# Sides of the feed-forward norm made within self-attention, early squares added by VectorE, the next group's norm one chunk ahead

## The chip, the cores and the metric

The kernel runs on one NeuronCore of a Trainium2 chip. The metric is the device time of one execution in microseconds, from launch to end; a profile gives in addition the span from the first to the last instruction on the core. Five engines work side by side, each on its own instruction queue: TensorE (PE) does matmuls, VectorE (DVE) and ScalarE (ACT) work element by element, GpSimd (POOL) too, and SyncE (SP) starts transfers. They wait for one another by semaphores. Matmul results land in PSUM[...]; everything else lives in SBUF.

## The reference

One perceiver block on 32 sequences of 64 positions and width 512, with a context of 1601 positions for each sequence; all in fp32:

```python
x = x + xattn(layernorm(x), ctx_1024, mask, rms_scale, q_w, kv_w, out_w)   # 4 heads of 128, one key/value head
x = x + attn(layernorm(x), WQ, WK, WV, WO)                                 # 16 heads of 32, causal
x = x + ffn(layernorm(x), W_fc, ln_w, ln_b, W_proj)

def ffn(x, W_fc, ln_w, ln_b, W_proj):          # 512 -> 2048 -> 512
    h = x @ absmean(W_fc).T                    # absmean: weights to -1, 0, 1
    h = gelu(h)                                # the exact one
    h = layernorm(h) * ln_w + ln_b             # over the 2048 hidden values
    return h @ absmean(W_proj).T
```

The change concerns the third line and the seam between the second and the third.

## The kernel before

The 2048 rows of x (32 sequences of 64) are 16 tiles `xs[0..15]` of 128 rows by 512, and stay in SBUF throughout. Cross-attention comes first and is not touched. A branch on a value read at run time picks between two forms of it, each followed by `rest`, which holds self-attention and the feed-forward part.

**Self-attention** (`self_attention`) runs a loop over i, the 16 tiles. Two tiles form a group (GA = 2). In turn i it normalises the probabilities of tile i (`normalise`: L1051 to L1053), turns them with TensorE's transposes (`turn`: `aptp` L1063, copies `wo` L1068 shared by ScalarE and VectorE), multiplies by the values (`mix`: `po` L1076), makes the scores and the exponentials of tile i + 1 (`exponentials`: `sc` L1028, `s` L1033, `amx` L1042, GpSimd's subtraction L1043, ScalarE's exponential L1046) and puts out tile i (`self_out`: `aout` L1090, addition to x L1093). Between these steps a generator fills in matmuls: queries, keys and values of the next group, or, for the last group (turns 14 and 15), `first_hidden`, the first 12 chunks of the feed-forward part's hidden layer. In turns 5, 7, 9 and 11 `ffn_input` makes the normalised and turned input of the feed-forward part for tiles 0 to 3. The comparisons that turn the weights into -1, 0, 1 (`compare`) are also put into these turns. All of these matmuls rotate through three PSUM banks (`ps_m`, tag "mm", of the pool `as_m`); two SBUF buffers (`raw`, tag "raw") serve first the weight pieces and then the squares of `first_hidden`.

**The feed-forward part** works on groups of four tiles (GT = 4, so 512 rows), 16 chunks of 128 hidden values a group (FC = 16), 64 chunks in all. `hidden(n)` makes chunk n: 8 matmuls `fh` (L912, the input in two parts, `fxh` and `fxl`, a rounded one and its remainder), Gelu into `bank` (L920), the square `fsq` (L922), then two running sums for the inner norm: `sums[0]` of the values on GpSimd (L926), and `sums[1]` of the squares (L927) on the engine given as `adder`: `nc.gpsimd` for the 12 chunks of `first_hidden`, `nc.vector` for the rest. `split(n)` multiplies the chunk by `ln_w` and divides it into two parts `hTh` and `hTl` on VectorE (L1204, L1205), two chunks ahead; three buffers hold each part. Then 8 matmuls `y` (L1225) add the chunk to the four output tiles.

The norm over the 2048 hidden values is not applied to them. What it does is put in at the end: `y` is scaled by the reciprocal deviation, and two row vectors, the **sides**, are added: `ln_w` times `W_proj`, weighted by minus mean times reciprocal deviation, and `ln_b` times `W_proj`. They are made at the start of `feed_forward`: `ln_w` and `ln_b` are loaded, divided into two parts (`lnp`, L876 and L877), and 16 matmuls `sides` (L1151) give 4 rows, which VectorE copies to `side` (L1153). `spread` (L1159) makes 128 equal rows of each of the two with matmuls against a small constant `pick`, and ScalarE copies them to `Wwb` (L1160). `others` (L1193, L1194) adds them to x, GpSimd the second one, VectorE the first one. `measure` (`fst` L1170) makes mean and deviation from the sums at chunk 8 of each group.

`ffn_input(t)` for tiles 4 to 15 is called in the loop over n, at the chunks that `inputs_at` names. It calls `centred` (statistics L110, L112, L114, GpSimd's power L115, normalised `xn_f` L117; two buffers), four transposes (`ftp` L902) and the two parts (L876, L877).

The order on each engine's queue is the work of a planner in the kernel language: it takes the instructions in program order as their priority, and moves a ready one forward where it reckons that the engine would be idle and a buffer is free. So `lnw`, `lnb` load and many statistics run far ahead of their place in the text. Once the order is fixed, each queue is served in order, and an instruction that waits holds those behind it.

Of the kernel before, what the change touches and what calls it, by code (L numbers as in the profile page):

```python
# [18 lines left out]
F32 = mybir.dt.float32  # L19
I32 = mybir.dt.int32  # L20

F32R = mybir.dt.float32r
# [6 lines left out]
P = 128  # L29
B, T, D = 32, 64, 512  # L30
S = 1601
NT = B * T // P
# [7 lines left out]
GT = 4  # L40
# [40 lines left out]
def perceiver_kernel(ctx: ExitStack, tc: tile.TileContext, a: dict, out: bass.AP):  # L81
# [25 lines left out]
    def centred(src, gain, eps, name):  # L107

        stats = small.tile([P, 6], F32, tag="stats", name=f"stats_{name}")
        nc.vector.bn_stats(stats, src)  # L110
        mv = small.tile([P, 2], F32, tag="mv", name=f"mv_{name}")
        nc.vector.bn_aggr(mv, stats)  # L112
        rs = small.tile([P, 1], F32, tag="rs", name=f"rs_{name}")
        nc.vector.tensor_scalar(rs, mv[:, 1:2], gain, eps, ALU.mult, ALU.add)  # L114
        nc.gpsimd.tensor_tensor(rs, rs, neghalf[:, 0:1], ALU.pow)  # L115
        xn = norm.tile([P, D], F32, tag="xn", name=f"xn_{name}")
        nc.vector.tensor_scalar(xn, src, mv[:, 0:1], rs, ALU.subtract, ALU.mult)  # L117
        return xn
# [764 lines left out]
    def rest(store, measured):  # L883
        st = ExitStack()
        fw = st.enter_context(tc.tile_pool(name="fw", bufs=1))
        wf = fw.tile([P, DC, FF], F32R, name="wf")
        wp = fw.tile([P, FC, D], F32R, name="wp")
        lnw = fw.tile([P, FC], F32, name="lnw")
        lnb = fw.tile([P, FC], F32, name="lnb")
        sums = fw.tile([P, 2, D], F32, name="sums")  # L890
        first = [fw.tile([P, DC, GT * P], F32R, name=f"fx{k}_0") for k in ("h", "l")]

        so_far = [None, None]

        def slot(n):
            return bank[:, n % FC // 4, n % 4 * D : (n % 4 + 1) * D]

        def ffn_input(t, to, ps_t, t_tag):
            xn = centred(xs[t], 1.0, 1e-5, f"f{t}")
            tp = ps_t.tile([P, DC, P], F32, tag=t_tag, name=f"ftp_{t}")  # L900
            for c in range(DC):
                nc.tensor.transpose(tp[:, c, :], xn[:, c * P : (c + 1) * P], ident)  # L902
            at = slice(t % GT * P, (t % GT + 1) * P)
            halves(to[0][:, :, at], to[1][:, :, at], tp)

        def hidden(n, fx, ps_m, m_tag, squares, sq_tag, adder):

            cols = slice(n % FC * P, (n % FC + 1) * P)
            ps = ps_m.tile([P, GT * P], F32, tag=m_tag, name=f"fh_{n}")
            for i, part in enumerate(fx):  # L910
                for c in range(DC):
                    nc.tensor.matmul(  # L912
                        ps,
                        wf[:, c, cols],
                        part[:, c, :],
                        start=(i == 0 and c == 0),
                        stop=(i == 1 and c == DC - 1),
                    )
            g = slot(n)
            nc.scalar.activation(g, ps, AF.Gelu)  # L920
            sq = squares.tile([P, D], F32, tag=sq_tag, name=f"fsq_{n}")
            nc.scalar.activation(sq, g, AF.Square)  # L922
            if n % FC == 0:
                so_far[:] = g, sq
            else:
                nc.gpsimd.tensor_tensor(sums[:, 0], so_far[0], g, ALU.add)  # L926
                adder.tensor_tensor(sums[:, 1], so_far[1], sq, ALU.add)  # L927
                so_far[:] = sums[:, 0], sums[:, 1]

        with ExitStack() as sa:  # L930
            done = self_attention(sa, wf, wp, first, ffn_input, hidden, measured)
        feed_forward(st, wp, lnw, lnb, sums, first, slot, ffn_input, hidden, done, store)
        st.close()

    def self_attention(st, wf, wp, first, ffn_input, hidden, measured):

        raw = st.enter_context(tc.tile_pool(name="raw", bufs=2))
        p1 = st.enter_context(tc.tile_pool(name="a1", bufs=1))
# [71 lines left out]
        def first_hidden():  # L1010

            for n in range(12):
                hidden(n, first, ps_m, "mm", raw, "raw", nc.gpsimd)
                if n % 2:
                    yield

# [88 lines left out]
        for i in range(NT):  # L1105
            g, t = divmod(i, GA)
            if t == 0:
                steps = heads(g + 1, xT) if g + 1 < groups else first_hidden()
            next(steps)
            normalise(i, s)  # L1110
            next(steps)
            if t == 0 and g + 2 < groups:
                xns = centred_group(g + 2)
            turn(i, s)
            next(steps)
            oT = mix(i)
            if i + 1 < NT:
                s = exponentials(i + 1)
            self_out(i, oT)
            for j in chores.get(i, ()):  # L1120
                compare(raw, j, piece_of(j))
            if t == GA - 1 and g + 2 < groups:
                xT = turned_group(g + 2, xns)
            if i in (5, 7, 9, 11):
                ffn_input((i - 5) // 2, first, ps_m, "mm")
        return 12

    def feed_forward(st, wp, lnw, lnb, sums, first, slot, ffn_input, hidden, done, store):
        fx = st.enter_context(tc.tile_pool(name="fx", bufs=1))
        ft = st.enter_context(tc.tile_pool(name="ft", bufs=3))  # L1130
        fq = st.enter_context(tc.tile_pool(name="fq", bufs=2))
        f1 = st.enter_context(tc.tile_pool(name="f1", bufs=1))
        ps_m = st.enter_context(tc.tile_pool(name="fs_m", bufs=2, space=PSUM))
        ps_t = st.enter_context(tc.tile_pool(name="fs_t", bufs=2, space=PSUM))
        ps_y = st.enter_context(tc.tile_pool(name="fs_y", bufs=GT, space=PSUM))
        nc.scalar.dma_start(lnw, a["ln_w"])
        nc.scalar.dma_start(lnb, a["ln_b"])
        pick = f1.tile([4, 2, P], F32, name="pick")
        nc.scalar.dma_start(pick, a["pick"])
        second = [fx.tile([P, DC, GT * P], F32R, name=f"fx{k}_1") for k in ("h", "l")]  # L1140
        inputs = [first, second]
        G = NT // GT
        last = G * FC


        lnp = f1.tile([P, FC, 4], F32R, name="lnp")
        for k, src in enumerate((lnw, lnb)):
            halves(lnp[:, :, 2 * k], lnp[:, :, 2 * k + 1], src)
        sides = ps_t.tile([P, D], F32, tag="tp", name="sides")
        for c in range(FC):  # L1150
            nc.tensor.matmul(sides[:4], lnp[:, c, :], wp[:, c, :], start=(c == 0), stop=(c == FC - 1))  # L1151
        side = f1.tile([4, D], F32, name="side")
        nc.vector.tensor_copy(side, sides[:4])  # L1153
        Wwb = f1.tile([P, 2, D], F32, name="Wwb")

        def spread():
            for k in range(2):
                ps = ps_t.tile([P, D], F32, tag="tp", name=f"spread_{k}")
                nc.tensor.matmul(ps, pick[:, k, :], side, start=True, stop=True)  # L1159
                nc.scalar.copy(Wwb[:, k], ps)  # L1160

        stats = {}

# [42 lines left out]
            return hi, lo  # L1206


        inputs_at = {n: GT + k for k, n in enumerate((1, 3, 5, 7, 11, 14, 17, 20, 27, 30, 33, 36))}
        made, ys = done, None  # L1210
        ahead = [split(0), split(1)]
        spread()
        for n in range(last):
            g, c = divmod(n, FC)
            if c == 0:
                ys = [ps_y.tile([P, D], F32, tag="y", name=f"y_{g}_{t}") for t in range(GT)]
            if made < last and (n >= 8 or n % 2 == 0):
                hidden(made, inputs[made // FC % 2], ps_m, "mm", fq, "sq", nc.vector)
                made += 1
            if n + 2 < last:  # L1220
                ahead.append(split(n + 2))
            parts = ahead.pop(0)
            for t in range(GT):
                for i, part in enumerate(parts):
                    nc.tensor.matmul(  # L1225
                        ys[t],
                        part[:, t, :],
                        wp[:, c, :],
                        start=(c == 0 and i == 0),
                        stop=(c == FC - 1 and i == 1),  # L1230
                    )
            if c == 8:
                measure(g)
            if 10 <= c < 10 + GT:
                others(g, c - 10)
            if n in inputs_at:
                t = inputs_at[n]
                ffn_input(t, inputs[t // GT % 2], ps_t, "tp")
            if c == FC - 1:
                for t in range(GT):  # L1240
                    i = g * GT + t
                    nc.vector.scalar_tensor_tensor(
                        xs[i], ys[t], stats[g][0][:, t : t + 1], xs[i], ALU.mult, ALU.add
                    )
                    store(i)
# [108 lines left out]
```

## Time and profile before

| | us |
|---|---|
| time, median of 3 runs | 984.78 (983.76 to 987.26) |
| the profiled execution's own time | 985.89 |
| its span | 984.1 |
| PE busy | 906.7 (92%) |
| DVE busy | 651.9 (66%) |
| ACT busy | 306.8 (31%) |
| POOL busy | 293.1 (30%) |
| `hidden` chunk 0 starts (PE) | 685.1 |
| `sides` on PE, start and length | 730.5, 3.87 |
| first `fst` (chunk 8 of group 0) | 772.0 |
| mean granted clock of TensorE | 0.98 |

In the views that follow, L912 and the like are lines of the kernel; `y<-wp,hTh` means that `y` is written and `wp` and `hTh` are read; x16 is a count. PE and PEld are TensorE's matmuls and its weight loads, which overlap. A wait is read as "engine, what waits, line <- engine, what it waited for". Busy matmuls are partly overlapped, so their spacing (0.23 us for these of 512 columns) and not their length (0.39 us) is what a chunk of work costs.

### The profile page before, as it was taken

What the parts mean: (1) busy time and instruction counts of PE and PEld (TensorE: products, weight loads), DVE (VectorE), ACT (ScalarE), POOL (GpSimd) and SP (SyncE); (2) the same over time, 40 slices, a digit from 0 to 9 for tenths busy, and PEclk for the clock granted to TensorE, in tenths of its full rate; (3) what the DMA queues carried; (4) which work ended last, traced back from release to release, by engine and by line L of the source; (5) the groups of instructions that cost most, each with busy time, mean ns of one, the idle gap of its engine ahead of it and who ended that gap; (6) DMA issues with size and microseconds to landing.
All of it is one profiled execution on the core that took longest, in us unless ns stands there. A gap on an engine that the chain in (4) does not pass through costs nothing.

```text
span 984.1 us, 13369 instructions
## 1 busy us (share of the span) xinstructions
PE 906.7 (92%) x4694; PEld 672.1 (68%) x4694; DVE 651.9 (66%) x1209; ACT 306.8 (31%) x694; POOL 293.1 (30%) x264
## 2 busy tenths in 40 slices
PE   4997889999999999988989999999979899999995
PEld 2786667777677766755566766766647688888884
DVE  4994456656565443499976666666439798886864
ACT  1112345455454532122222222222622233333330
POOL 3554222323222221011011111111757454443330
PEclk9999899999999999999999999999999999999998
DMA  6266664876776550023310000000000010010101
GB/s 198 65 206 168 196 190 136 278 235 206 235 208 213 149 182 24 21 86 87 87 43 1 1 1 1 1 2 1 1 1 1 1 43 1 1 44 1 43 1 46
DMA packets 60964, 83.74 MB, mean 85 GB/s; under 512 B 11060, under 2 KB 34136, under 8 KB 60888
## 3 DMA queue, kind: packets, MB, share of 16 engines
q1 hardware_dynamic: 57568, 80.60, 27.3%
q10 hardware_dynamic: 3320, 2.20, 0.7%
q8 instruction: 39, 0.64, 0.3%
q14 instruction: 37, 0.30, 0.1%
HBM read 74.38 MB, written 4.19 MB: 80 GB/s over the span
## 4 chain that ended last, share of the span: by engine, by line
PE 62%; DVE 14%; POOL 4%; issue 3%; DMA 3%; ACT 3%; SPq 1%; POOLq 0%; DVEq 0%; ACTq 0%
PE y L1225 10%; PE fh L912 10%; PE kvp L382 9%; PE aV L1000 5%; PE xo L504 5%; PE aWQ L984 4%; PE aWK L984 4%; PE lgp L424 3%; PE enc L488 3%; DVE s L1033 3%; DMA nat<-in_ctx_dram 2%; PE aout L1090 2%; PE po L1076 1%; DVE amx L1042 1%; PE sc L1028 1%
## 5 line engine op out<-in xcount | busy, mean ns | idle before, releaser
L382 PE MATMUL kvp<-wkv,ct 128*128 128x256 f32 x576 | 140.8, 391 | 4.4 <-ACT kv L389 4.4
L382 PEld LDWEIGHTS kvp<-wkv,ct 128*128 128x128 f32 x576 | 111.5, 197 | 27.9 <-issue 7.3
L926 POOL TENSOR_TENSOR sums<-sums,bank 128x512 f32<-128x512 f32 x56 | 77.2, 1378 | 90.9 <-ACT bank L920 90.7
L1225 PE MATMUL y<-wp,hTh 128*128 128x512 f32 x256 | 102.7, 401 | 0.6 <-DVE hTh L1204 0.6
L1225 PE MATMUL y<-wp,hTl 128*128 128x512 f32 x256 | 100.7, 393 | 0.7 <-DVE hTl L1205 0.7
L1043 POOL TENSOR_TENSOR s<-s,amx 128x1024 f32<-128x1024 f32 x16 | 30.6, 1913 | 226.0 <-DVE amx L1042 226.0
L920 ACT ACTIVATE bank<-fh 128x512 f32<-128x512 f32 x64 | 38.1, 599 | 154.0 <-PE fh L912 154.0
L912 PE MATMUL fh<-fxh,wf 128*128 128x512 f32 x256 | 73.1, 407 | 6.3 <-issue 4.8
L912 PE MATMUL fh<-fxl,wf 128*128 128x512 f32 x256 | 71.4, 401 | 0.0
L1033 DVE SCALAR_TENSOR_TENSOR s<-sc,cmask 64x1024 f32<-64x1024 f32 x32 | 39.1, 1222 | 44.5 <-PE sc L1028 44.1
L927 DVE TENSOR_TENSOR sums<-sums,fsq 128x512 f32<-128x512 f32 x46 | 54.6, 1186 | 19.5 <-ACT fsq L922 19.4
L1000 PE MATMUL aV<-bank,axT 128*128 128x512 f32 x128 | 62.2, 631 | 4.4 <-DVE KT L991 4.4
L389 ACT ACTIVATE kv<-kvp,rstd 128x256 f32<-128x256 f32 x72 | 33.2, 469 | 92.8 <-PE kvp L382 54.6
L504 PE MATMUL xo<-wo,encT 128*128 128x512 f32 x128 | 59.7, 609 | 2.1 <-ACT encT L497 2.0
L1090 PE MATMUL aout<-bank,aoT 128*128 128x512 f32 x128 | 59.2, 605 | 0.7 <-ACT aoT L1084 0.7
L984 PE MATMUL aWQ<-axT,bank 128*128 128x256 f32 x256 | 58.3, 381 | 1.5 <-ACT axT L967 1.5
L912 PEld LDWEIGHTS fh<-fxh,wf 128*128 128x128 f32 x256 | 47.1, 190 | 18.3 <-issue 6.8
L1205 DVE SCALAR_TENSOR_TENSOR hTl<-bank,lnw,hTh 128x512 fp32r<-128x512 f32 x64 | 55.9, 874 | 5.3 <-PE y L1225 1.1
L191 PE MATMUL q<-xT,wq 128*128 128x256 f32 x256 | 58.2, 386 | 0.0
L984 PE MATMUL aWK<-axT,bank 128*128 128x256 f32 x256 | 57.9, 379 | 0.0
L1225 PEld LDWEIGHTS y<-wp,hTh 128*128 128x128 f32 x256 | 48.2, 188 | 13.8 <-DVE hTh L1204 1.4
L912 PEld LDWEIGHTS fh<-fxl,wf 128*128 128x128 f32 x256 | 48.9, 191 | 12.5 <-issue 0.8
(156 smaller groups left out, 1625.9 us busy)
## 6 DMA issues: line engine op xcount, KB each, us to landing
nat<-in_ctx_dram SPq DMA_DIRECT2D x64, 256.0 KB, 5.1
ct<-in_ctxT_dram SPq DMA_DIRECT2D x7, 768.0 KB, 4.8
xraw<-in_x_dram SPq DMA_DIRECT2D x16, 256.0 KB, 2.7
x<-in_x_dram SPq DMA_DIRECT2D x32, 128.0 KB, 4.9
qs<-bank SPq DMA_DIRECT2D x32, 128.0 KB, 3.1
raw_g<-in_W_fcT_dram SPq DMA_DIRECT2D x16, 256.0 KB, 3.7
raw_g<-in_W_projT_dram SPq DMA_DIRECT2D x16, 256.0 KB, 4.4
raw_q<-in_W_fcT_dram SPq DMA_DIRECT2D x16, 256.0 KB, 3.0
```

Source lines behind the costliest of these rows:

```text
L191: nc.tensor.matmul(ps.rearrange("p b t -> p (b t)"), wq[:, c, h, :], xT[:, c, :], start=(c == 0), stop=(c == DC - 1),)
L382: nc.tensor.matmul(ps.rearrange("p k h -> p (k h)"), cts[p][:, c, j * P : (j + 1) * P], wkv[:, c].rearrange("p k h -> p (k h)"), start=(c ...
L504: nc.tensor.matmul(o, encT[:, h].rearrange("p s t -> p (s t)"), wo[:, h, :], start=(h == 0), stop=(h == NH - 1),)
L912: nc.tensor.matmul(ps, wf[:, c, cols], part[:, c, :], start=(i == 0 and c == 0), stop=(i == 1 and c == DC - 1),)
L926: nc.gpsimd.tensor_tensor(sums[:, 0], so_far[0], g, ALU.add)
L927: adder.tensor_tensor(sums[:, 1], so_far[1], sq, ALU.add)
L984: nc.tensor.matmul(ps[:, m, :], ws[w][:, c, (m0 + m) * P : (m0 + m + 1) * P], xT[:, c, :], start=(c == 0), stop=(c == DC - 1),)
L1000: nc.tensor.matmul(ps, xT[:, c, i * P : (i + 1) * P], ws["WV"][:, c, :], start=(c == 0), stop=(c == DC - 1),)
L1033: nc.vector.scalar_tensor_tensor(s[half], sc[half, :, :, half].rearrange("p r m k -> p (r m) k"), DK**-0.5, cmask[half].unsqueeze(1).to_br ...
L1090: nc.tensor.matmul(ps, oT[:, c, :], ws["WO"][:, c, :], start=(c == 0), stop=(c == DC - 1))
L1205: nc.vector.scalar_tensor_tensor(lo, g, w, hi.bitcast(F32), ALU.mult, ALU.subtract)
L1225: nc.tensor.matmul(ys[t], part[:, t, :], wp[:, c, :], start=(c == 0 and i == 0), stop=(c == FC - 1 and i == 1),)
```

## The change

Four things, in one function after the other:

- The loads of `ln_w`, `ln_b` and `pick`, the division into `lnp`, the `sides` matmuls with their copy, and `spread` move from `feed_forward` to self-attention. The loads stand at the head of `rest`, `lnp` ahead of self-attention, `sides` at the end of turn 14 and `spread` at the end of turn 15. `sides` and `spread` use self-attention's "mm" banks; `side` takes one of the two "raw" buffers; `Wwb` no longer has SBUF of its own but lies in `wkv`, the key and value weights of cross-attention.
- The squares of the first 12 chunks are added by VectorE instead of GpSimd.
- `ffn_input` is cut in two: `ffn_input` is now the norm alone, `ffn_turned` the transposes and the two parts. In the loop over chunks the norm of a tile is called at one chunk and its turning at the next chunk.
- `inputs_at` names chunks 0, 2, 4, 6 in place of 1, 3, 5, 7 for the second group's tiles, so their turnings stay at chunks 1, 3, 5, 7. The others keep their chunk for the norm, and their turning goes one chunk later.

```diff
@@ rest
+        lnp = fw.tile([P, FC, 4], F32R, name="lnp")
+        pick = fw.tile([4, 2, P], F32, name="pick")
+        nc.scalar.dma_start(lnw, a["ln_w"])
+        nc.scalar.dma_start(lnb, a["ln_b"])
+        nc.scalar.dma_start(pick, a["pick"])
+
+        Wwb = wkv.rearrange("p c k h -> p (c k h)").rearrange("p (k d) -> p k d", k=2)
+
+        def sides(psum, tag, pool, s_tag):
+            ps = psum.tile([P, D], F32, tag=tag, name="sides")
+            for c in range(FC):
+                nc.tensor.matmul(
+                    ps[:4], lnp[:, c, :], wp[:, c, :], start=(c == 0), stop=(c == FC - 1)
+                )
+            side = pool.tile([P, D], F32, tag=s_tag, name="side")
+            nc.vector.tensor_copy(side[:4], ps[:4])
+
+            def spread():
+                for k in range(2):
+                    ps = psum.tile([P, D], F32, tag=tag, name=f"spread_{k}")
+                    nc.tensor.matmul(ps, pick[:, k, :], side[:4], start=True, stop=True)
+                    nc.scalar.copy(Wwb[:, k], ps)
+
+            return spread
...
-        def ffn_input(t, to, ps_t, t_tag):
-            xn = centred(xs[t], 1.0, 1e-5, f"f{t}")
+        def ffn_input(t):
+            return centred(xs[t], 1.0, 1e-5, f"f{t}")
+
+        def ffn_turned(t, xn, to, ps_t, t_tag):
             tp = ps_t.tile([P, DC, P], F32, tag=t_tag, name=f"ftp_{t}")
...
         with ExitStack() as sa:
+            for k, src in enumerate((lnw, lnb)):
+                halves(lnp[:, :, 2 * k], lnp[:, :, 2 * k + 1], src)
@@ self_attention
-                hidden(n, first, ps_m, "mm", raw, "raw", nc.gpsimd)
+                hidden(n, first, ps_m, "mm", raw, "raw", nc.vector)
...
             if i in (5, 7, 9, 11):
-                ffn_input((i - 5) // 2, first, ps_m, "mm")
+                k = (i - 5) // 2
+                ffn_turned(k, ffn_input(k), first, ps_m, "mm")
+            if i == NT - 2:
+                spread = sides(ps_m, "mm", raw, "raw")
+            if i == NT - 1:
+                spread()
@@ feed_forward
-        nc.scalar.dma_start(lnw, a["ln_w"])
-        nc.scalar.dma_start(lnb, a["ln_b"])
...
-        sides = ps_t.tile([P, D], F32, tag="tp", name="sides")
-        for c in range(FC):
-            nc.tensor.matmul(sides[:4], lnp[:, c, :], wp[:, c, :], start=(c == 0), stop=(c == FC - 1))
...
-        inputs_at = {n: GT + k for k, n in enumerate((1, 3, 5, 7, 11, 14, 17, 20, 27, 30, 33, 36))}
-        made, ys = done, None
+        inputs_at = {n: GT + k for k, n in enumerate((0, 2, 4, 6, 11, 14, 17, 20, 27, 30, 33, 36))}
+        made, ys, waiting = done, None, []
         ahead = [split(0), split(1)]
-        spread()
...
-            if n in inputs_at:
-                t = inputs_at[n]
-                ffn_input(t, inputs[t // GT % 2], ps_t, "tp")
+            for t, xn in waiting:
+                ffn_turned(t, xn, inputs[t // GT % 2], ps_t, "tp")
+            waiting = [(inputs_at[n], ffn_input(inputs_at[n]))] if n in inputs_at else []
```

More of the change, by code (lines that the diff above doesn't have):

```diff
@@ L930, in rest, with self_attention @@
         with ExitStack() as sa:
-            done = self_attention(sa, wf, wp, first, ffn_input, hidden, measured)
-        feed_forward(st, wp, lnw, lnb, sums, first, slot, ffn_input, hidden, done, store)
+            for k, src in enumerate((lnw, lnb)):
+                halves(lnp[:, :, 2 * k], lnp[:, :, 2 * k + 1], src)
+            done = self_attention(sa, wf, wp, first, ffn_input, ffn_turned, hidden, sides, measured)
+        feed_forward(st, wp, lnw, Wwb, sums, first, slot, ffn_input, ffn_turned, hidden, done, store)
         st.close()
-    def self_attention(st, wf, wp, first, ffn_input, hidden, measured):
+    def self_attention(st, wf, wp, first, ffn_input, ffn_turned, hidden, sides, measured):
         raw = st.enter_context(tc.tile_pool(name="raw", bufs=2))
@@ L1124, in self_attention, with feed_forward @@
             if i in (5, 7, 9, 11):
-                ffn_input((i - 5) // 2, first, ps_m, "mm")
+                k = (i - 5) // 2
[4 more added lines that the diff above has]
+                spread()
         return 12
-    def feed_forward(st, wp, lnw, lnb, sums, first, slot, ffn_input, hidden, done, store):
+    def feed_forward(st, wp, lnw, Wwb, sums, first, slot, ffn_input, ffn_turned, hidden, done, store):
         fx = st.enter_context(tc.tile_pool(name="fx", bufs=1))
@@ L1131, in feed_forward @@
         fq = st.enter_context(tc.tile_pool(name="fq", bufs=2))
-        f1 = st.enter_context(tc.tile_pool(name="f1", bufs=1))
         ps_m = st.enter_context(tc.tile_pool(name="fs_m", bufs=2, space=PSUM))
@@ L1135, in feed_forward @@
         ps_y = st.enter_context(tc.tile_pool(name="fs_y", bufs=GT, space=PSUM))
-        nc.scalar.dma_start(lnw, a["ln_w"])
-        nc.scalar.dma_start(lnb, a["ln_b"])
-        pick = f1.tile([4, 2, P], F32, name="pick")
-        nc.scalar.dma_start(pick, a["pick"])
         second = [fx.tile([P, DC, GT * P], F32R, name=f"fx{k}_1") for k in ("h", "l")]
@@ L1143, in feed_forward @@
         last = G * FC
-        lnp = f1.tile([P, FC, 4], F32R, name="lnp")
-        for k, src in enumerate((lnw, lnb)):
-            halves(lnp[:, :, 2 * k], lnp[:, :, 2 * k + 1], src)
-        sides = ps_t.tile([P, D], F32, tag="tp", name="sides")
-        for c in range(FC):
[L1151 to L1160, printed above, removed]
         stats = {}
```

## The prediction

> **What bounds the kernel now.** I read the busy time by stage first, then the chain that ended last in order of time, then the waits of the stage that looked worst, then the tiles concerned. The view by windows (window; busy time and count of PE, weight loads, DVE, ACT, POOL; granted clock; DMA share; GB/s):
>
> ```profile
> 684.00:703.00 19.00, 17.63 (x128) 12.68 (x127) 8.83 (x13) 12.06 (x20) 13.45 (x11) 1.00 0.00 1
> 703.00:722.00 19.00, 16.05 (x74) 11.29 (x76) 7.41 (x10) 9.59 (x17) 13.99 (x11) 0.95 0.00 1
> 722.00:738.00 16.00, 13.64 (x68) 6.57 (x59) 7.54 (x12) 2.69 (x5) 4.90 (x5) 0.95 0.00 0
> 738.00:772.00 34.00, 27.87 (x119) 21.42 (x118) 29.64 (x43) 4.99 (x9) 23.30 (x18) 0.95 0.00 1
> 772.00:834.00 62.00, 62.00 (x284) 50.43 (x283) 56.18 (x75) 20.08 (x33) 29.87 (x22) 1.00 0.08 17
> ```
>
> From 772 us on TensorE has no gap, and just before 684 us (attention of tiles 12 and 13) it has none either: 17.10 of 17.10 us busy in the window 651.4 to 668.5. Whatever moves the point at 772 us moves the end one for one; whatever the change does later than that is covered by a full TensorE. Between 684 and 772 us TensorE is idle or slow. The chain in order of time says on what (start, us, what):
>
> ```profile
> 713.95 1.25 POOL sums L927
> 715.28 1.27 POOL sums L927
> 716.58 0.63 ACT fsq L922
> ...
> 718.92 2.74 PE fh L912 x8
> 721.66 1.88 PE po L1076 x28
> ...
> 729.77 0.70 DVE x L1093
> 730.52 3.87 PE sides L1151 x16
> 734.39 0.93 PE fh L912 x4
> 735.32 1.91 PE spread L1159 x4
> 737.23 1.14 PE fh L912 x4
> ```
>
> GpSimd's additions of squares (L927) release ScalarE's squares, and only behind those come the copies that TensorE's `po` of the last tile needs. Then `sides` and `spread` lie open on the chain. The waits from 690 to 740 us (waiter, cause, total us, times, longest):
>
> ```profile
> ACT fsq L922 <- POOL sums L927: 5.0, 4, 1.9
> PE po L1076 <- ACT wo L1068: 2.8, 1, 2.8
> PE sides L1151 <- DVE x L1093: 1.7, 1, 1.7
> POOL x L1193 <- ACT Wwb L1160: 11.1, 1, 11.1
> ```
>
> The 738 to 772 window has another limit: DVE is busy 29.64 of 34 us. Its operations there are stretched while GpSimd works. The tiles (ns min/median/max, first and last start, forms), and the two lines of the timeline where it ends in an open stall of TensorE:
>
> ```profile
> L927 DVE TENSOR_TENSOR sums<-sums,fsq x46: 676/1287/1793, 741.2 to 955.8; 128x512 f32<-128x512 f32 x46
> L927 POOL TENSOR_TENSOR sums<-sums,fsq x10: 1263/1288/1447, 695.4 to 725.4; 128x512 f32<-128x512 f32 x10
> L1204 DVE TENSOR_SCALAR hTh<-bank,lnw x64: 470/475/1520, 724.2 to 968.2; 128x512 fp32r<-128x512 f32 x64
> ...
> 767.20 0.68 DVE L876 CAST fxh<-ftp 128x512 fp32r<-128x512 f32 x1
> 768.09 2.05 PE L912 MATMUL fh<-fxh,wf 128*128 128x512 f32 x4 [4.77 <-issue]
> ```
>
> **What the Trainium skill says.** "SBUF — State Buffer", section "Who interferes with whom": a DVE instruction in a two-port mode, or with two SBUF inputs beside a GpSimd instruction that reads SBUF, and GpSimd lock each other out for a whole instruction. The trace agrees: the same `hTh` takes 470 ns alone and up to 1520, the addition 676 and up to 1793. "GPSIMD Engine Reference", section 3.1: the addition is about twice as slow on GpSimd as on VectorE; here 1288 against 676 ns. "TensorE: Matmul & The Clock Gate", Part 1: an idle window of about 3.4 us halves the clock; the granted clock is 0.95 here and 1.00 around, after open waits of 2.8 us and 4.77 us. "Perfetto Trace Analysis", section "Optimization Strategy": repeating gaps can mean too few buffers; it bears on the fourth rival.
>
> **TensorE's account from 685.1 to 738.2 us.** A chunk of the hidden layer (8 matmuls) takes 1.86 us when nothing is open. Work in these 53.1 us: hidden chunks 0 to 12, 13 x 1.86 = 24.2; two turnings of probabilities 2 x 1.04 = 2.1; two `po` 2.0; one `sc` 1.15; two `aout` 2 x 3.6 = 7.2; `sides` 3.87; `spread` 1.91; four matmuls of `y` 0.93. Sum 43.4 us. So 9.7 us are idle or slow clock: 1.4 at 695 us (hidden chunk 4 for a bank), 2.8 before `po`, some 1.8 of slow matmuls behind it (2.74 instead of 1.86, 1.88 instead of 1.0), 0.7 before `aout`, 1.7 before `sides`, and about 1.3 around `spread`, small gaps for the rest.
>
> **Part 1, sides and spread.** All their PE work stays, 3.87 and 1.91 us, so this is no saving of work. `sides` needs the weights `wp`, ready at 509 us, and goes behind the output of tile 14, before hidden chunk 6. There TensorE would otherwise reach the end of its chunks before the softmax of tile 15: that softmax is done at 711.4 us (L1053), and with 3.73 to 3.87 us put in at 704 us chunks 6 to 9 end at 715.3 instead of before 713, the turning and chunk 10 follow without a gap, and `po` starts about 718. `spread` follows `aout` of tile 15 and covers the 0.7 us addition L1093, which waits now behind splits and the `lnp` conversions (0.66, 0.17, 1.24, 0.17 = 2.24 us of DVE at 723.6 to 727). Those four now run behind two 8 KB loads on ScalarE's queue, which the trace already has at 386 us; the `pick` load (0.51 us of the queue at 723.57) joins them. That is beside TensorE work with DVE waiting 2.77 us for `xo` at 386 us: nothing, or at worst 2.2 us if put in front of a norm. The copy `side` (0.68 us DVE) and the copies `Wwb` (2 x 0.59 us ACT) move along. `Wwb` takes the space of the finished cross-attention weights: no wait.
>
> **Part 2, squares by VectorE.** Eleven GpSimd additions of about 1.29 us (14.1 us of its 27.4 in 684 to 722) become eleven on DVE. The trace has them there only in the later stage: 0.68 us alone, 1.19 mean, 1.79 at most, so 7.5 to 19.7 us; I take 1.1, 12 us. DVE is busy 16.2 of 38 us in the two windows, so there is room. GpSimd then needs 1.3 to 1.7 us a chunk for the other sum instead of 2.56, below TensorE's 1.86. ScalarE's waits of 5.0 us go. Behind such a waiting square stand, on ScalarE's queue, the next Gelu (which frees a bank for TensorE) and the copies for `po`. New wait: `side` keeps one of the two `raw` buffers from tile 14 to `spread`, so a square waits for the addition before it: 0.63 + 0.7 to 1.5 = 1.3 to 2.1 us a chunk against 1.86. I take +0.7 us in all for the last six chunks; bounds 0 and 1.5.
>
> Of the 9.7 us I leave 2.0 (the wait of chunk 4, in part, and that before `aout`) and the 0.7: a gain of **7.0 us**, bounds 4 and 9.
>
> **Part 3, the norm ahead.** No operation is added or removed. The statistics run far ahead already (14 of the 16 before 690 us) and two normalised tiles are held, so in chunks 0 to 8 TensorE's wait on `xn_f` is nil. Later groups lie under a full TensorE. I take 0, bounds -1 and +1.5 us (a turning that no longer has DVE's conversion stuck behind a norm).
>
> **Chunks 0 to 8 (738 to 772).** DVE's stretch above the shortest of the kind sums to 8.6 us: `hTh` three times 1.0, `hTl` 0.84 and 0.85, additions 1.08, 0.88, 1.11 and 0.45, `xn_f` 0.4. GpSimd's additions of `Wwb` (1.28 to 1.75 us each) begin at 737.93, 0.3 us before the rest of `y`; after the change `Wwb` comes about 2 us before it. That takes one or two stretches: **1.3 us**, bounds 0 and 6 (all, if `spread` is put into a gap earlier and GpSimd does its six free additions before). The conversion at 767.2, late by DVE's backlog, is what is late next.
>
> Sum 7.0 + 0 + 1.3 = 8.3 us. The span of 984.1 (execution 985.89) goes to 975.8; the median of the runs shown, 984.78, to **976.5 us**. The profiled execution is 1.1 us above that median, so differences are carried over, not absolute values.
>
> **Rivals.** (A) As above: 973 to 979.5, 52%. (B) `spread` goes ahead and the lock of chunks 0 to 8 dissolves: 7 + 6 = 13 us, 971.5; for it, GpSimd is busy 2.5 us in 17 before tile 14 and could take the additions early; against, TensorE has no gap there. 13%. (C) DVE becomes the bound: the eleven additions at 1.8 us and the one `raw` buffer keep chunks 6 to 11 at 2.1 us, part 1 and 2 shrink to 4 us: 980.8, 15%. (D) Nothing measurable: `sides` lies open in tile 14 (3.9 us) because the softmax of tile 15 gets slower by the additions in front of it: 984.8, 9%. (E) Slower: the planner starts `sides` in any gap after 509 us, and its bank, one of the three that all of self-attention's matmuls rotate through, stays taken for several tiles. With two banks, an evacuation (0.59 us ACT, 0.69 DVE) is open for each of some six tiles per turn: 3.6 us a tile. It decides from 8.3/3.6 = 2.3 tiles of holding; at four, 14.4 - 8.3 = 6 us slower, 991, 11%. For it: the weight comparisons run 100 us ahead of their place, so this planner does move work; against: TensorE has no gap in tiles 12 and 13, and the first hidden chunk, ready at 652 us, was not moved ahead of 685. That the squares don't move at all isn't possible: the engine is named.
>
> Range by these: A, C, two thirds of B and half of D, 969.5 to 984.0; A alone 973 to 979.5. What a measurement can tell from no change is 0.3%, 3 us. Faster by more: 0.52 + 0.13 + 0.15 = 0.80; same 0.09; slower 0.11.
>
> **What would show it.** Right: no L927 on GpSimd, no ACT wait on it, `sides` near 704 us with `po` of tile 15 straight after chunk 10, clock 1.00 from 703 to 738, chunk 0 of `y` complete some 7 us earlier, 738 to 772 about as long as before. Wrong: `sides` before 690 us with longer turns of attention (E); ACT waiting for DVE at L922 by over 5 us (C); the stage from `y` to the first `fst` longer than 34 us, the gain lost behind DVE.

## The result and the profile after

The changed kernel takes 982.33 us (median of 22 runs, 977.02 to 986.41); the kernel before, beside it on the same chip, 986.49 us (22 runs, 981.76 to 993.38). The ratio is 0.9946 with a 95% interval of 0.9928 to 0.9965: faster by 0.54%, about 5.3 us by the ratio and 4.2 us by the medians. The forecast was a gain of 8.3 us; the predicted 976.5 us is missed by 5.8 us, of which 1.7 are the higher median of the kernel before in these runs (986.49 instead of 984.78) and 4.1 a gain that was forecast too large. The range, 969.5 to 984.0 us, holds the time.

The profiled execution of after took 977.61 us with a span of 975.9 us (before: 985.89 and 984.1). Those 8.2 us of span must not be read as the gain. Self-attention's first matmul starts at 387.3 us before and at 383.8 us after, behind code of cross-attention that is the same in both; over the kernels below the same code ended anywhere between 383.4 and 389.2 us. So each trace is measured by stages with TensorE's own marks: self-attention from its first query matmul to the first `fh` of chunk 0; **stage A** from there to the fifth matmul of `y` of chunk 0; **stage B** from there to the first `fst` (chunk 8); the **tail** from there to the end.

| kernel | first query matmul at | self-attention | A | B | A + B | tail |
|---|---|---|---|---|---|---|
| before | 387.3 | 297.8 | 53.07 | 33.79 | 86.86 | 212.12 |
| after | 383.8 | 298.1 | 48.21 | 33.66 | 81.87 | 212.13 |

The change itself is worth 86.86 - 81.87 = 5.0 us, all but 0.1 of it in stage A. That agrees with the ratio.

Busy time by windows of the kernel after, cut at the places that answer to those shown of before (columns as there):

```profile
680.80:699.80 19.00, 17.65 (x127) 12.66 (x126) 13.58 (x17) 12.05 (x20) 9.07 (x6) 1.00 0.00 1
699.80:718.80 19.00, 17.88 (x83) 11.57 (x82) 12.65 (x17) 9.32 (x16) 8.38 (x6) 1.00 0.00 1
718.80:730.00 11.20, 10.17 (x53) 5.53 (x52) 6.71 (x9) 2.87 (x5) 3.91 (x4) 1.00 0.00 0
730.00:763.80 33.80, 28.31 (x119) 21.70 (x118) 28.99 (x43) 5.16 (x9) 20.54 (x17) 0.90 0.00 1
```

The third window is 11.2 us long, where before it took 16. In the second TensorE is busy 17.88 of 19 us instead of 16.05, at clock 1.00 instead of 0.95. VectorE took the squares (13.58 and 12.65 us instead of 8.83 and 7.41). The fourth window is as long as it was to 0.2 us, with VectorE busy 28.99 us of 33.8; its granted clock is 0.90 instead of 0.95. Behind it TensorE is busy 62.00 of 62.00 us, as before.

What TensorE still waits for in stage A, and its open stall in stage B, from its timeline in the kernel after (start, us, engine, line, what; in brackets the idle time before it and its cause):

```profile
691.54 1.19 PE L938 MATMUL fh<-fxh,wf 128*128 128x512 f32 x4 [0.74 <-ACT bank L946]
694.28 1.16 PE L938 MATMUL fh<-fxh,wf 128*128 128x512 f32 x4 [0.61 <-DVE wo L1096]
715.21 1.21 PE L938 MATMUL fh<-fxh,wf 128*128 128x512 f32 x4 [1.08 <-ACT bank L946]
721.67 3.70 PE L1118 MATMUL aout<-bank,aoT 128*128 128x512 f32 x8 [1.03 <-ACT aoT L1112]
759.37 2.04 PE L938 MATMUL fh<-fxh,wf 128*128 128x512 f32 x4 [4.77 <-issue]
```

`sides`, not shown, starts without a wait at 701.55 us. The four waits of stage A sum to 3.46 us; the stall of 4.77 us before chunk 16 (the first chunk of the second group) in stage B is to the hundredth the one that stood at 768.09 us before. The chain of work that ended last in the kernel after shows what stands behind the wait at 715.21:

```profile
710.73 1.58 DVE sums L953
...
713.00 1.02 DVE sums L953
...
714.67 0.49 ACT bank L946
715.21 2.13 PE fh L938 x8
```

Before, GpSimd's additions stood in this place, and `po` behind them. Now VectorE's stand there, with 1.58 and 1.02 us, and behind them a Gelu that frees a bank.

### The profile page after: what moved, and what is told of

Its sections match the earlier page's. It is cut to its first block, busy times and chain, and to the rows that moved or that the text cites. A ratio compares the mean times of both kernels' runs of the same rounds, so it can differ in the third digit from the quotient of the medians.

```text
span 975.9 us, 13372 instructions
## 1 busy us (share of the span) xinstructions
PE 901.0 (92%) x4694; PEld 670.1 (69%) x4694; DVE 663.4 (68%) x1220; ACT 306.9 (31%) x694; POOL 281.4 (29%) x253
## 4 chain that ended last, share of the span: by engine, by line
PE 64%; DVE 14%; DMA 3%; issue 3%; POOL 3%; ACT 3%; SPq 1%; ACTq 0%; DVEq 0%; POOLq 0%
PE y L1235 11%; PE fh L938 11%; PE kvp L382 10%; PE xo L504 5%; PE aV L1028 4%; PE aWQ L1012 4%; PE aWK L1012 4%; PE enc L488 3%; PE lgp L424 3%; PE aout L1118 3%; DVE s L1061 3%; DMA nat<-in_ctx_dram 1%; PE sc L1056 1%; PE pt L473 1%; DVE amx L1070 1%
## 5 line engine op out<-in xcount | busy, mean ns | idle before, releaser
L953 DVE TENSOR_TENSOR sums<-sums,fsq 128x512 f32<-128x512 f32 x56 | 67.2, 1201 | 23.8 <-ACT fsq L948 23.7
L1012 PEld LDWEIGHTS aWQ<-axT,bank 128*128 128x128 f32 x256 | 48.0, 190 | 12.9 <-issue 3.8
```

The source lines that it names most:

```text
L1012: nc.tensor.matmul(ps[:, m, :], ws[w][:, c, (m0 + m) * P : (m0 + m + 1) * P], xT[:, c, :], start=(c == 0), stop=(c == DC - 1),)
```

## The experiments

Each ratio is against runs of the kernel before on the same chip; e5 and e7 have 4 runs each, the others 9 to 22. The stages of a kernel, in us, come from its one profile:

| kernel | first query matmul at | self-attention | A | B | A + B | tail | time | ratio (95%) |
|---|---|---|---|---|---|---|---|---|
| e12 sides only | 387.4 | 298.6 | 50.30 | 33.64 | 83.94 | 212.37 | 983.76 | 0.9968 (0.9943 to 0.9993) |
| e2 squares only | 389.2 | 298.1 | 50.03 | 34.63 | 84.66 | 215.86 | 984.95 | 0.9966 (0.9950 to 0.9982) |
| e3 norm only | 385.4 | 298.9 | 53.22 | 34.44 | 87.66 | 211.95 | 987.77 | 1.0010 (0.9986 to 1.0034) |
| e1 squares back | 388.1 | 298.7 | 50.25 | 33.66 | 83.91 | 212.42 | 983.12 | 0.9948 (0.9921 to 0.9975) |
| e4 no norm ahead | 385.9 | 300.9 | 48.23 | 33.65 | 81.88 | 213.69 | 983.13 | 0.9947 (0.9925 to 0.9970) |
| e5 side elsewhere | 388.3 | 298.7 | 48.05 | 33.20 | 81.25 | 212.00 | 977.22 | 0.9912 (0.9886 to 0.9938) |
| e6 spread early | 385.5 | 300.2 | 51.00 | 28.44 | 79.44 | 212.00 | 978.85 | 0.9923 (0.9896 to 0.9949) |
| e7 no second row | 383.4 | 298.7 | 48.24 | 25.67 | 73.91 | 212.31 | 973.37 | 0.9888 (0.9861 to 0.9915) |
| e8 conversion on ScalarE | 385.5 | 300.3 | 48.24 | 30.81 | 79.05 | 212.02 | 978.66 | 0.9937 (0.9909 to 0.9965) |
| e9 second row later | 386.1 | 297.9 | 48.22 | 25.67 | 73.89 | 225.57 | 987.31 | 0.9999 (0.9975 to 1.0022) |
| e10 e9 with e5 and e8 | 385.0 | 300.1 | 48.04 | 26.32 | 74.36 | 224.25 | 986.64 | 0.9995 (0.9977 to 1.0013) |
| e11 before, second row later | 388.8 | 298.4 | 53.07 | 25.65 | 78.72 | 228.83 | 994.99 | 1.0064 (1.0037 to 1.0092) |

Stage A repeats to 0.03 us where squares and sides are moved (48.21, 48.23, 48.24, 48.24, 48.22) and to 0.15 us where neither is (53.07, 53.22, 53.07). The tail mostly repeats within 0.5 us. Stage B is less steady: e2, whose edit doesn't touch it, has 34.63 us there instead of 33.79. The start of self-attention wanders over 6 us and its length over 3 (300.9 us in e4, whose edit doesn't touch it). So stage A tells tenths of a microsecond apart that the ratio can't; in stage B a difference under 1 us is not read as an effect of the edit.

### Which part brought it: e1, e2, e3, e4, e12

e1 is the kernel after with the squares given back to GpSimd:

```diff
-                hidden(n, first, ps_m, "mm", raw, "raw", nc.vector)
+                hidden(n, first, ps_m, "mm", raw, "raw", nc.gpsimd)
```

> The changed kernel with the squares of the first 12 chunks added by GpSimd again (sides moved and norm ahead remain). Measured from the first fh matmul of chunk 0 to the ninth... to the fifth y matmul of chunk 0 (stage A: 53.1 us before, 48.2 after) and from there to the first fst (stage B: 33.8 and 33.7). Theory 1 (squares and sides need each other: with GpSimd's 2.56 us a chunk and only one raw buffer left beside side, ScalarE waits longer than before): stage A 51 to 54 us, ACT waiting on GpSimd's L953 over 5 us, time as the kernel before or up to 1 us slower. Rival (moving sides into the hole is the whole gain, the squares only moved): stage A 48 to 49 us and the time of the changed kernel.

e2 is the kernel before with that same line turned the other way, and nothing else.

> The kernel before with only the squares of the first 12 chunks on VectorE. Theory 1: the holes before po and behind it go (2.8 + 1.8 us of the 53.1), stage A 48.5 to 50 us, stage B 33.8, time 3 to 4.5 us under the kernel before. Rival (sides are the gain): stage A 52 to 53 us, time within 1.5 us of before. If both are right in part, stage A lies at 50 to 52.

e3 is the kernel before with `ffn_input` cut in two and the norm called one chunk ahead, and nothing else.

> The kernel before with only the norm cut from its turning and called one chunk ahead. Both theories: stage A 53.1 us, stage B 33.3 to 34.3 us, later stages unchanged (212.1 us from the first fst to the end), time within 1 us of before. A rival in which the norm ahead is worth something gives stage B under 32.5 us.

e4 is the kernel after without that:

```diff
-        inputs_at = {n: GT + k for k, n in enumerate((0, 2, 4, 6, 11, ...))}
+        inputs_at = {n: GT + k for k, n in enumerate((1, 3, 5, 7, 11, ...))}
...
-            for t, xn in waiting:
-                ffn_turned(t, xn, inputs[t // GT % 2], ps_t, "tp")
-            waiting = [(inputs_at[n], ffn_input(inputs_at[n]))] if n in inputs_at else []
+            if n in inputs_at:
+                t = inputs_at[n]
+                ffn_turned(t, ffn_input(t), inputs[t // GT % 2], ps_t, "tp")
```

> The changed kernel with the norm called in the chunk of its turning again (1, 3, 5, 7). Both theories: stage A 48.2 us, stage B 33.3 to 34.3 us, 212.1 us behind it, time within 1 us of the changed kernel. A rival in which the norm ahead is worth something gives stage B over 35 us.

e12 is e4 with e1's line: the kernel before with the sides moved, and nothing else.

> The kernel before with only the sides moved (loads, lnp, sides, spread, Wwb in the place of wkv); squares on GpSimd and the norm as before. Stage A 50.0 to 50.6 us as with the norm ahead (50.25), stage B 33.7; time 2 to 4 us under the kernel before. A rival in which the norm ahead matters beside GpSimd's squares: stage A over 51.5.

In stage A the sides alone bring 53.07 - 50.30 = 2.77 us, the squares alone 3.04, both together 4.86: 0.95 less than the sum. e1 and e2 came out between what stood against each other: 50.25 us in e1, although ScalarE waits 6.1 us there for GpSimd's sums, and 50.03 us in e2, where 50 to 52 stood for both being right in part. So neither part needs the other, and neither is the whole gain. e12 came out as expected.

The norm ahead brings nothing that can be seen in A and B (e4 against after: 48.23 and 33.65 against 48.21 and 33.66; e3 alone: 0.15 us slower in A and 0.65 in B, where up to 34.3 us had been expected, and a ratio that includes 1). The tail of e4 is 1.6 us longer than that of after, 0.9 of it one wait of TensorE for VectorE's output additions (L1252). The kernel before and e12, which have no norm ahead either, show no such wait, so its cause stays open.

Why the two bring less together than their sum shows in a view of stage A alone, in before, with the sides alone (e12), with the squares alone (e2) and in after (columns as above):

```profile
685.12:738.19 53.07, 46.39 (x258) 30.28 (x257) 22.69 (x33) 24.34 (x41) 32.52 (x25) 0.97 0.00 1
685.99:736.29 50.30, 44.70 (x258) 29.43 (x257) 21.78 (x29) 24.32 (x41) 34.46 (x26) 1.00 0.00 1
687.28:737.31 50.03, 45.47 (x258) 29.45 (x257) 34.02 (x44) 23.88 (x41) 20.89 (x14) 1.00 0.00 1
681.90:730.11 48.21, 44.71 (x259) 29.41 (x257) 31.87 (x40) 24.25 (x41) 21.46 (x15) 1.00 0.00 1
```

The length of the stage less TensorE's busy time is what TensorE waits: 6.68, 5.60, 4.56 and 3.50 us. The sides take 1.08 us off it, the squares 2.12, both 3.18: the waits add up. What doesn't add up is the busy time of the same matmuls: 1.69 us less with the sides, 0.92 with the squares, 1.68 with both. Before, the matmuls behind the wait of 2.81 us before `po` were slow (2.74 us for 8 `fh` and 1.88 for 28 `po`). With the sides alone that wait is gone, with the squares alone 0.37 us of it are left; the slow matmuls can be taken away only once. The split has its own scatter: e11 repeats before (46.40 us busy) and e1 repeats e12 (44.68), but e3, with the same stage A as before, was busy 47.55 us and waited 5.67.

Each move alone leaves a line of sums in the chain. With the sides alone (e1 here, whose stage A is that of e12) it is GpSimd's, almost without a gap from 713 to 727 us, with `aout` behind it. Three of its lines:

```profile
722.34 1.24 POOL sums L952
723.58 1.24 POOL sums L953
...
728.58 3.70 PE aout L1118 x8
```

With the squares alone (e2) TensorE arrives early at the end of its chunks, and VectorE makes the softmax of tile 15 and then four sums of squares in one run from 714.26 to 720.92 us, each of them stretched to some 1.6 us. The end of that run in the chain of e2:

```profile
717.63 1.60 DVE sums L927
...
719.33 1.59 DVE sums L927
...
720.95 0.44 DVE wo L1068
...
721.82 1.68 PE po L1076 x30
```

Here the copies `wo`, for which `po` waits, stand behind VectorE's sums.

e2's ratio is worth more than its span: its tail is 3.7 us longer than before, and that lies in one window, with TensorE full (columns as above; the granted clock is 0.80):

```profile
772.00:792.00 20.00, 20.00 (x82) 16.72 (x81) 12.92 (x22) 5.59 (x10) 5.12 (x5) 0.80 0.00 1
```

The 0.80 is a mean. In windows of 2 and 3 us the granted clock is 0.50 from 767 to 778 us, 0.70 from 778 to 781 and 1.00 behind that.

### What is left in stage A: e5

`side` lies in the half of `Wwb` that `spread` writes only after it has been read, and takes no "raw" buffer:

```diff
-            side = pool.tile([P, D], F32, tag=s_tag, name="side")
+            side = Wwb[:, 1]
```

> The changed kernel with side kept in the place that the second row of Wwb takes later, so both raw buffers stay with the squares. Theory (my term of 0.7 us for the one raw buffer, bounds 0 and 1.5): stage A (first fh matmul of chunk 0 to the fifth y matmul of chunk 0) 46.7 to 48.0 us in place of 48.2, stage B (from there to the first fst) 33.7, time up to 1.5 us under the changed kernel. Rival (ScalarE's wait on VectorE lies beside TensorE's other work): stage A 48.2, no change.

Stage A goes from 48.21 to 48.05, B from 33.66 to 33.20. In A TensorE waits no less than in after (3.65 us in all, 3.50 in after). In B VectorE's last conversion (L876) starts as late as in after, 28.36 us into the stage and 28.37; the difference lies in the matmuls behind the stall, which take 3.95 us up to `fst` instead of 4.40. So the rival holds: the one remaining buffer costs 0.2 us at most. The ratio, 0.9912 from 4 runs, is better than that explains; its interval overlaps that of after (0.9928 to 0.9965), and the stages show no place for more.

### What limits stage B: e6, e7, e8

e7 leaves out the second row, `ln_b` times `W_proj`:

```diff
             x = xs[g * GT + t]
-            nc.gpsimd.tensor_tensor(x, x, Wwb[:, 1], ALU.add)
             nc.vector.scalar_tensor_tensor(
```

> The changed kernel without GpSimd's additions of the second side to x; the output lacks the row of ln_b times W_proj. Theory 1 (the lock): stage B 28 to 31 us, hTh of chunks 3 to 10 near 480 ns, stage A unchanged at 48.2, time 3 to 6 us under the changed kernel. Rival (VectorE's own work): stage B over 32.5 us.

Stage B falls from 33.66 to 25.67 us, by 8.0, more than theory 1 had expected, and nothing else moves. The chain of e7 in that stage is TensorE alone but for one gap of 0.38 us. Three of its lines:

```profile
733.27 0.44 PE ftp L928 x4
733.70 1.86 PE fh L938 x8
735.57 3.73 PE y L1234 x16
```

Ten additions of 1.28 us and more on GpSimd, an engine with time to spare, cost the stage 8 us. VectorE's instructions are as many as before, but shorter: 43 with 22.71 us busy in the window from 730.0 to 755.5 us of e7, 43 with 28.99 us in that from 730.0 to 763.8 of after (shown above).

```profile
730.00:755.50 25.50, 25.12 (x117) 20.13 (x116) 22.71 (x43) 4.92 (x8) 8.66 (x8) 1.00 0.00 1
```

How the 8.0 us are made up shows at the end of the stage. VectorE's last conversion there, in after and in e7, from the timelines:

```profile
758.48 0.68 DVE L876 CAST fxh<-ftp 128x512 fp32r<-128x512 f32 x1
...
752.69 0.68 DVE L876 CAST fxh<-ftp 128x512 fp32r<-128x512 f32 x1
```

And the `fh` of chunk 16 that follow it, from the chains of after (two lines) and e7 (two lines):

```profile
759.37 2.04 PE fh L938 x4
761.84 1.71 PE fh L938 x4
...
753.58 1.17 PE fh L938 x4
754.98 0.93 PE fh L938 x4
```

The conversion starts 28.37 us into stage B in after and 22.37 us in e7, so 6.0 us are VectorE's. The other 2.0 are TensorE's: from the first of these `fh` to `fst` it needs 4.40 us behind the stall of 4.77 us in after, and 2.41 us in e7, which has no such stall.

A rival would be that GpSimd's queue makes VectorE late, because the power L115 that the norm needs stands there behind an addition. The timeline of after speaks against it: behind the instruction at 731.01 us no wait stands before any of VectorE's until 760.49 us, so GpSimd's queue doesn't hold it up there; the time lies inside its instructions. This is the lock between GpSimd and VectorE that the Trainium skill describes ("SBUF — State Buffer", section "Who interferes with whom"), now with a price measured on the end of the stage and not only on the single instruction. The trace agrees in detail: beside GpSimd `sums`, which reads SBUF twice, takes up to 1.79 us instead of 0.68, while `fxl`, which reads PSUM (`ftp`) and SBUF, takes 0.68 us beside the addition at 739.72 us too.

e6 makes `spread` straight behind `sides`, at the end of turn 14:

```diff
             if i == NT - 2:
-                spread = sides(ps_m, "mm", raw, "raw")
-            if i == NT - 1:
-                spread()
+                sides(ps_m, "mm", raw, "raw")()
```

> The changed kernel with spread right behind sides, at the end of turn 14, so that Wwb is there some 15 us earlier and GpSimd can add it to six tiles before the y of chunk 0. Theory 1 (the lock by those six additions stretches VectorE in chunks 0 to 8): stage B 29.5 to 32 us in place of 33.7, stage A 47.5 to 49. Rival (VectorE's own work and its order bind chunks 0 to 8, the lock only fills what would be waiting): stage B 33 us or more, time within 1 us of the changed kernel.

GpSimd then makes six of the additions inside stage A, in one run. Timeline of e6 (GpSimd, and TensorE's `spread`):

```profile
710.37 1.98 PE L911 MATMUL spread<-side,pick 4*128 4x512 f32 x4 [0.77 <-DVE side L906]
...
713.05 7.95 POOL L1202 TENSOR_TENSOR x<-x,wkv 128x512 f32<-128x512 f32 x6 [4.47 <-ACT wkv L912]
```

B falls by 5.2 us to 28.44, more than theory 1 had it, and A rises by 2.8 to 51.00, which it had not: `spread` no longer covers a wait at the end of tile 15 (0.56 us now) but opens one of 0.77 us in tile 14. A + B is 2.4 us shorter than after. Stage A of e6 as a window:

```profile
685.66:736.66 51.00, 46.31 (x259) 30.56 (x257) 33.27 (x40) 24.32 (x41) 28.10 (x19) 0.97 0.00 1
```

Of A's rise 1.2 us are waits (4.69 us in all instead of 3.50), and 1.6 us are a longer busy time of the same 259 matmuls (46.31 us instead of 44.71). The four chunks behind `spread` take 9.19 us, where four take 7.4 when nothing is open. What slowed them wasn't shown by a run.

e8 lets ScalarE write the rounded part of the turned input, and VectorE only the remainder:

```diff
-            halves(to[0][:, :, at], to[1][:, :, at], tp)
+            hi, lo = to[0][:, :, at], to[1][:, :, at]
+            nc.scalar.copy(hi, tp)
+            nc.vector.tensor_tensor(lo, tp, hi.bitcast(F32), ALU.subtract)
```

> The changed kernel with the rounded part of each turned input (fxh) written by ScalarE instead of VectorE, in self-attention and in the loop over chunks. Theory 2 (what is late in chunks 0 to 8 is the conversion queued on VectorE, and 4 x 0.68 us of its work): stage B 28 to 31.5 us, the wait of 4.8 us before the fh of chunk 16 under 2 us. Theory 1 (the lock by GpSimd alone): stage B over 33 us. Stage A 48.2 in both.

B falls by 2.8 us to 30.81, inside the range of theory 2, but the stall doesn't fall under 2 us: it moves from one half to the other. Waits of e8 in this stage:

```profile
PE fh L940 <- DVE fxl L932: 3.9, 1, 3.9
```

TensorE waits for the remainder that VectorE still makes, 3.9 us instead of 4.77. As in e5 to e7 the tail doesn't change. The edit lies in self-attention too, which took 300.3 us; it took 300.9 in e4 without it, so a cost there is neither shown nor excluded. The ratio of e8, 0.9937, can't be told from that of after.

### Can the additions be put under a full TensorE: e9, e10, e11

e7 shows a prize of 8 us, and behind the first `fst` TensorE has no gap for 62 us. In e9 the two additions of `others` change places; the first one needs the statistics of chunk 8, so the second one, now behind it, can't be moved ahead into stage B:

```diff
             x = xs[g * GT + t]
-            nc.gpsimd.tensor_tensor(x, x, Wwb[:, 1], ALU.add)
             nc.vector.scalar_tensor_tensor(
...
             )
+            nc.gpsimd.tensor_tensor(x, x, Wwb[:, 1], ALU.add)
```

> The changed kernel with the two additions of others in the other order: VectorE's first, which needs the statistics of chunk 8, then GpSimd's second row, which therefore can't be moved ahead of them. Theory 1 (the lock binds chunks 0 to 8, and a full TensorE hides it afterwards): stage B (fifth y matmul of chunk 0 to the first fst) 25.5 to 27.5 us in place of 33.7, from the first fst to the end 212 to 213, stage A 48.2, time 6 to 8.5 us under the changed kernel. Rival (the lock costs the same wherever it falls, since VectorE is busy 56 of 62 us after the first fst): 218 us or more behind the first fst, time within 2 us of the changed kernel.

e10 is e9 with the edits of e5 and e8 on top.

> The changed kernel with the second row added behind the first, side kept in the place of Wwb's second row, and fxh written by ScalarE: three edits of the runs so far together. If they add up: stage A 48.0, stage B 24.7 to 25.7 us (TensorE's own work there is 24.7), 212 us behind, time 8 to 9.5 us under the changed kernel. If the lock was the only limit of stage B, the conversion on ScalarE adds nothing to the second row's 25.5 to 27.5.

e11 is the kernel before with that swap and nothing else.

> The kernel before with only the two additions of others in the other order. Theory 1: the lock was there all the same and needs nothing of the change: stage A 53.1, stage B 25.5 to 27.5 in place of 33.8, 212 to 213 us behind it, time 6 to 8.5 us under the kernel before, so more than the change itself brought. Rival (without the change's earlier Wwb the stage is bound elsewhere): stage B over 31 us.

In stage B theory 1 is right: it falls by 8.0 us to 25.67 as with e7, in e11 too (to 25.65), where the rival had over 31 us. So the lock needs nothing of the change. Behind the first `fst` theory 1 is wrong: the tail rises by 13.4 us in e9 and by 16.7 in e11. For e9 that is its rival, and more than the rival had: e9 is some 5 us slower than the changed kernel by the two ratios (0.9999 and 0.9946), and e11 slower than the kernel before. e10 gains 1.3 us of the tail back and has 0.7 us more in B, so its edits do not add up. TensorE's waits of e9 from the first `fst` to the end, where the kernel after has none at all:

```profile
PE y L1235 <- DVE x L1252: 6.5, 8, 1.7
PE y L1235 <- DVE hTl L1216: 1.8, 3, 1.1
```

These are 8.3 of the 13.4 us. The other 5.1 are a longer busy time: from the first `fst` to the last matmul TensorE is busy 206.06 us for the same 913 matmuls that take 200.93 in after. The two windows, after and e9:

```profile
763.77:964.70 200.93, 200.93 (x913) 163.48 (x911) 164.85 (x227) 58.97 (x96) 79.40 (x57) 1.00 0.07 17
757.93:972.37 214.44, 206.06 (x913) 163.44 (x911) 176.24 (x226) 59.11 (x96) 97.38 (x67) 0.99 0.07 16
```

VectorE is busy 11.4 us longer there, with one instruction fewer. How much of the 5.1 us is TensorE's clock wasn't separated. One of the windows of e9, at the first change of group, has VectorE busy 19.62 of 20 us:

```profile
776.00:796.00 20.00, 17.12 (x71) 12.73 (x70) 19.62 (x29) 4.93 (x8) 7.24 (x6) 0.97 0.15 36
```

The chain of e9 says how it comes: from 761.9 to 793.9 us it is VectorE nearly alone, and it begins with VectorE's own additions of the first side (L1204). These take as long in after (3.15 us for three). What follows doesn't: at this place `sums` takes 0.68 us in after and `hTh` 0.48.

```profile
761.89 3.12 DVE x L1204 x3
765.01 1.72 DVE sums L953
766.74 1.44 DVE hTh L1215
...
788.82 1.40 DVE x L1252 x2
...
793.92 0.73 PE y L1235 x2
```

All 16 second-row additions now lie in the tail, four in a bunch for each group, where after had ten of them before the first `fst` and the other six 10 to 28 us apart. A VectorE with 56 of 62 us busy has no room for a bunch: it falls behind, the last addition of the output (`x` L1252), which frees the banks of `y`, comes late, and TensorE, full until then, stops.

## Why the prediction was right or wrong

**What bounds the kernel** (idle or slow TensorE from 684 to 772 us, a full one behind it, so that what is gained at the first `fst` is gained at the end): right. A + B fell by 5.0 us and the tail moved by 0.01. But the rule holds in one direction only. The prediction said that whatever the change does later is covered by a full TensorE; e9 shows that a full TensorE covers only what leaves VectorE its slack, and that was 6 us in 62.

**Part 1** (sides and spread, in a hole before the softmax of tile 15): the place was right, `sides` without a wait at 701.55 us, 19.7 us behind the first `fh`, where "near 704" was 18.9 behind it. What follows was put too early: chunk 6 started at 704.72 us before, so 3.73 us more move the end of chunk 9 to 716.3 us and not to 715.3, and so it came (31.2 us behind the first `fh` in both). `po` came 35.4 us behind the first `fh` and not 33, for this reason and because chunk 10 had a gap of 1.08 us in front of it. The `lnp` conversions cost nothing that can be seen above the 6 us by which the start of self-attention wanders.

**Part 2** (squares by VectorE): right in kind. ScalarE's waits for the sums fall from 5.0 us in all to 2.1 (three times, 1.1 at most), and the eleven additions on VectorE took 1.04 us in the mean and 1.58 at most, where 1.1 had been taken.

**Their sum, 7.0 us, is the step that was mis-sized: 4.86 us measured**, inside the bounds of 4 to 9. The account of 43.4 us of TensorE work left 2.0 us of idle time and 0.7 for the one raw buffer, 2.7 in all. It is 48.21 - 43.4 = 4.8 us: 3.5 of waits and 1.3 of matmuls that are spaced wider (44.71 us busy). The 2.0 named two waits, of chunk 4 (0.74 measured) and before `aout` (1.03), and was right for these. Not on the list were 0.61 us before 694.28, for VectorE's copy of `wo`, and 1.08 us before chunk 10, which comes from the work that part 2 moved: two stretched sums in a row on VectorE hold ScalarE's squares and the Gelu behind them. The wider spacing had no term at all. The term for the raw buffer was too large, 0.2 us at most by e5. The mistake of method is that all waits of one chain were counted as gone because their first cause was gone; the engine that took the work over brought shorter ones in the same places.

**Part 3** (norm ahead): 0 predicted; e4 measures 0.01 us in A + B.

**Chunks 0 to 8:** 1.3 us predicted, 0.13 measured, inside 0 to 6. `Wwb` did come 2.1 us ahead of the rest of `y`, and one of ten additions went out of the window with it. VectorE did reach its last conversion sooner, by 0.64 us, half of what was forecast: 28.37 us into the stage instead of 29.01 (28.33 to 28.37 in e1, e4, e5 and e12, which have the sides moved, 29.34 in e2 and e3, which have not). But the stall before chunk 16 is the same 4.77 us, and the matmuls behind it took 4.40 us instead of 3.89, which ate 0.51 of the 0.64; e5, with the same stall, had 3.95. The price of the lock as a whole, 8.6 us summed up from stretched instructions, looks close to the 8.0 of e7, but by luck: e7 takes 6.3 us off VectorE's busy time, since GpSimd's own sums still stretch some of its instructions, and 2.0 of its 8.0 us are matmuls that are no longer slow behind a stall, which the prediction did not count.

**The rivals.** (A) has the mechanism but not the size: 982.33 us lies outside its 973 to 979.5, and the gain, 5.0 us by stages and 5.3 by the ratio, lies at its smallest (984.78 - 979.5 = 5.3). By stages it is nearer to (C), 4 us, than to the 8.3 of (A); the stated range holds it because it reaches on to (C) and half of (D). (B), the lock dissolved because the planner moves `spread` ahead, did not come by itself; made by hand (e6) it gives 5.2 us in B and takes 2.8 in A, so that 6 us free of charge were too much. (Its 971.5 us should be 984.78 - 13 = 971.8.) (C), VectorE as the bound, holds in part: its sums do stand on the chain at 710 to 714 us, but they took 1.04 us and not 1.8, ScalarE waits 2.1 us for them, not over 5, and the clock in the second window is 1.00. (D) and (E) fell: nothing lies open at `sides`, the planner did not start it early, and self-attention takes 298.1 us against 297.8. The remark on too few buffers belongs to (E), the fifth rival, and not to the fourth.

## What to carry to other kernels

Two cures for one hole need not add up: price the second on what the first leaves, and look for the engine that inherits the removed waits. Read a gain of half a per cent by a stage between two marks of the busiest engine, not by the span, which moved here by 3.5 us in code that was not touched; and split a stage into waits and busy time, since matmuls behind a stall can be slow. An addition on a "free" GpSimd is paid by VectorE, so it belongs where VectorE has slack, which is not the same place as where TensorE is full. e6 and e8 are 2.4 and 2.8 us shorter than the changed kernel in A + B, but their ratios can't be told from its own, and whether the two add up was not run.

## What the runs showed that was not expected

- Ten GpSimd additions (some 14 us of GpSimd's time) lengthen a stage of TensorE and VectorE by 8.0 us (e7), 2.0 of them by slow matmuls behind the stall that they cause. Sixteen of them, in place of six, behind the first `fst`, where VectorE is busy 56 of the first 62 us, cost 12 to 17 us (e9 to e11).
- In e2 TensorE's granted clock stayed at 0.50 for some 11 us behind a stall of 5.09 us, although TensorE was busy throughout from 767.54 us; the 16 `fst` matmuls of one column each fall into that time. That one execution's tail was 3.7 us longer. Others with the same idle stage had a clock of 0.99 or 1.00 in the 20 us behind the first `fst`, so one profile's tail can't be compared without its clock.
- The same code before self-attention ended between 383.4 and 389.2 us from one kernel to the next.
